# dt times the input on VectorE out of PSUM, a uniform four-state add on GpSimd, and a third softplus at a place of its own, in a scan on one Trainium2 core

## The chip, the cores and the metric

The kernel runs on one core of a Trainium2 chip. The core has five engines with a queue each: TensorE (PE: matmuls, with PEld for its weight loads), VectorE (DVE), ScalarE (ACT), GpSimd (POOL) and SyncE (SP, which only issues DMAs here). Each takes its instructions in the order in which the program gives them, and a semaphore wait holds up everything behind it on the same engine. The metric is the time of one execution in device microseconds.

## The reference, cut to what matters

The network has four layers on 8 images of 192 channels by 64 x 64 pixels. Layers 0 and 2 hold a selective scan in four directions; layers 1 and 3 have no recurrence. The change is in the scan alone, which runs 16 times (8 images, 2 layers). For each direction, with R rows that are projected to `dt` and N = 16 states:

```python
dt = softplus(einsum('kcr,bkrl->bkcl', dt_proj_w, dts) + dt_proj_b)
A = -exp(A_log)
def step(h, inp):
    dt_t, B_t, C_t, x_t = inp
    h = h * exp(dt_t[..., None] * A) + (dt_t * x_t)[..., None] * B_t[:, :, None, :]
    return h, einsum('bkcn,bkn->bkc', h, C_t)
```

So per position and channel: one softplus, one product dt x input, 16 exponentials (the decay), 16 products with B, a recurrence for each of 16 states, 16 products with C, and the sum over the 16 states. All of it is float32.

## The kernel before

**Tiling.** `scan_layer` (lines 99 to 449) works on units. A unit is 128 channel rows (block v = 0, 1 or 2; block 2 holds the last 64 channels of two directions) by Q = 512 positions; it has 4 sub-blocks of 128 positions, and its states are the tile `da` of 128 x (4 x 16 x 128) floats. Three units, v = 0, 1, 2, share one stretch of positions and make a chunk. A scan has two directions d of 8 chunks, so 16 chunks or 48 units; the whole kernel has 768 units and 256 chunks.

**What one unit costs each engine.**
- ACT: `steps_b` (L217) takes the softplus of the projected dt out of a PSUM bank into `dts`; `decay` (L244) makes the 16 exponentials of 128 x 512; `turn` copies (L231, L234) bring the transposed product into SBUF; `cut` (L253, L254) saves and clears the first column of each sub-block. Softplus and Exp are in different function tables, so the change from one to the other needs an ACT_TABLE_LOAD.
- POOL: `steps_c` (L221) makes `dtx` = dt x input. `times_c` (L317 to L322) multiplies a sub-block's 16 states by C (L319, 128 x 2048) and then adds the last n states to others (L322), so that fewer are left for PE: n = 4 in the first two sub-blocks, n = 3 in the last two.
- PE: `turn` transposes `dtx` (L229); `fill` (L287) makes dtx x B for half a sub-block into a PSUM tile `u`, of which there are two; `add_up` (L337) sums the states into `py` by matmuls with the identity, 12 for a unit, and one of half width (L342) for the state that POOL left out in two sub-blocks. `py` has one buffer.
- DVE: `scan` (L303, L305, L308) runs the recurrence on half a sub-block, 128 x 1024, in place on `da`, 8 times a unit; `diagonals_b` (L196) spreads B for the next chunk, 4 times a chunk; `finish` (L352 in direction 0, L356 in direction 1) takes `py` out.

**The order.** It is written by hand (`tc.manual_schedule()`): no scheduler moves anything. The loop at L394 takes a unit k in eight slots j. A slot issues scan(k, j), the POOL work of the sub-block behind it, `fill` for the next slot, then the rest: `finish` of unit k-2 and `turn` of unit k+1 in slot 2, `add_up` for unit k-1 with as many matmuls as SUM[v][j] says, and a part of the decay of unit k+1 (DECAY). What prepares the next chunk is spread over the three units: `steps_a` (PE, the projection of dt, into a `misc` PSUM bank, of which there are two) for two units in slot 4 of v = 0; then, in slot 1 of v = 1, one burst of three softplus with the third `steps_a` in its midst, since that one needs a bank that the first softplus frees.

**The start of a scan** (L369 to L393) makes dt, dtx, the B diagonals and the decay of unit 0 before the loop. The decay of unit 0 is made in two halves of the sub-blocks, so that DVE can begin its first scans after the first half.

**What limits how far an engine may run ahead.** `fill` for slot j+1 needs the `u` tile of slot j-1, so that scan must be over. The first matmul of `add_up` for unit k-1 needs `finish` of unit k-2 (the one buffer of `py`) and POOL's product for the last sub-block of unit k-1. The decay of unit k+1 needs the third buffer of `da`, so the last `add_up` of unit k-2.

Of the kernel before, what the change touches and what calls it, by code (L numbers as in the profile page):

```python
# [7 lines left out]
F32 = mybir.dt.float32  # L8
AF = mybir.ActivationFunctionType
ALU = mybir.AluOpType  # L10
# [4 lines left out]
P = 128  # L15
# [5 lines left out]
Q = 512  # L21
NS = 16
SB = 128
NB = Q // SB
# [16 lines left out]
def tile_net(ctx: ExitStack, tc: tile.TileContext, a: dict, out: bass.AP):  # L41
    nc = tc.nc
# [56 lines left out]
    def scan_layer():  # L99
# [5 lines left out]
        with (  # L105
# [9 lines left out]

            nck = T // Q


            NP = 12
            units = [  # L120
                (d, i, i if d == 0 else nck - 1 - i, v)
# [59 lines left out]
            def diagonals_a(m, o):  # L181

                pt = misc()
                rows = slice(o * CB, o * CB + NS)
                for i, cols in windows():
                    nc.tensor.transpose(  # L186
                        pt[:, i * NS : (i + 1) * NS], xd[m][rows, cols], ident[rows, rows]
                    )
                bts[m, o] = pt[:, : 8 * NS].rearrange("p (i n) -> p i n", n=NS)
                dg[m, o] = sw.tile([P, 8, NS // 2, 32], F32, tag=f"dg{o}", name=f"dg{o}")  # L190
# [13 lines left out]
            def steps_a(k):  # L204

                d, i, c, v = units[k]
                x = xd[k // 3][:, 0:Q]
                pz = pzs[k] = misc()
                if v < 2:
                    r = slice(v * CB, (v + 1) * CB)  # L210
                    nc.tensor.matmul(pz, wdt[r, d, 0, :], x[r], start=True, stop=True)
                else:
                    nc.tensor.matmul(pz, wdt[:, d, 1, :], x, start=True, stop=True)  # L213

            def steps_b(k):
                dts[k] = sw.tile([P, Q], F32, tag="dt", name="dt", bufs=4)
                nc.scalar.activation(dts[k], pzs.pop(k), AF.Softplus)  # L217

            def steps_c(k):
                dtx[k] = sw.tile([P, Q], F32, tag="dtx", name="dtx")  # L220
                nc.gpsimd.tensor_tensor(dtx[k], dts[k], vt[k // 3][:, units[k][3], :], ALU.mult)  # L221

            def turn(k):

# [92 lines left out]
            def times_c(k, g):  # L317
                h = das[k][:, NB - 1 - g if units[k][0] else g]
                nc.gpsimd.tensor_tensor(h, h, cts.pop((k, g)), ALU.mult)  # L319
                n = NS - NP if g < 2 else NS - NP - 1  # L320
                to = h[:, NP - n : NP]
                nc.gpsimd.tensor_tensor(to, to, h[:, NS - n : NS], ALU.add)  # L322

            def load_y(k):
                d, i, c, v = units[k]
# [6 lines left out]
            def add_up(count):  # L332

                for k, n in to_add[:count]:
                    if n == 0:
                        py[k] = sp.tile([P, Q], F32, tag="py", name="py")
                    nc.tensor.matmul(  # L337
                        py[k], ident, das[k][:, :, n, :], start=(n == 0), stop=(n == NP - 1)
                    )
                    if n == 8:  # L340
                        s = slice(0, NB // 2) if units[k][0] else slice(NB // 2, NB)
                        nc.tensor.matmul(  # L342
                            py[k][:, s.start * SB : s.stop * SB], ident, das[k][:, s, NP, :],
                            start=False, stop=False,
                        )
                del to_add[:count]

            def finish(k):
# [10 lines left out]
            nu, nm = len(units), len(units) // 3  # L359


            SUM = ((1, 0, 1, 2, 0, 2, 1, 2), (2, 2, 1, 1, 1, 2, 2, 2), (2, 1, 1, 2, 2, 2, 2, 2))
            DECAY = {2: (0, 3), 3: (3, 7), 4: (7, 9), 5: (9, 12), 6: (12, 16)}

            def has(k):
                return 0 <= k < nu
# [7 lines left out]
            load_v(1)  # L374
            steps_b(0)
            steps_c(0)
            steps_a(2)
            steps_b(1)
            diagonals_a(0, 0)
            steps_b(2)  # L380
            for r in range(2):
                diagonals_b(0, 0, r)
                load_c(0, r)
# [1 line left out]
            for s in (slice(0, NB // 2), slice(NB // 2, NB)):  # L385
                decay(0, 0, NS, s)
                cut(0, s)
                if s.start == 0:
                    steps_c(1)
                    diagonals_a(0, 1)  # L390
                    fill(0, 0)
            for r in range(2):
                diagonals_b(0, 1, r)  # L393
            for k in range(nu + 2):  # L394
                m, v = divmod(k, 3)
                ahead = 0 <= m + 1 < nm
                for j in range(8):
                    if v == 1 and j == 3 and 0 <= m + 2 < nm:
                        load_v(m + 2)
                    if has(k):  # L400
                        scan(k, j)
                    if j == 7:
                        if has(k + 1):
                            cut(k + 1)
                        if has(k):
                            keep(k)
                    if j % 2 == 0:
                        kk, g = (k, j // 2 - 1) if j else (k - 1, 3)
                        if has(kk):
                            times_c(kk, g)  # L410
                        if has((4 * kk + g + 3) // 4):
                            load_c(*divmod(4 * kk + g + 3, 4))
                    if j == 5 and has(k + 2):
                        steps_c(k + 2)
                    kk, jj = (k, j + 1) if j < 7 else (k + 1, 0)
                    if has(kk):
                        fill(kk, jj)
                    if j == 2:
                        if has(k - 2):
                            finish(k - 2)  # L420
                        if has(k - 1):
                            load_y(k - 1)
                        if has(k + 1):
                            turn(k + 1)
                    if ahead and (v, j) == (0, 4):

                        steps_a(k + 3)
                        steps_a(k + 4)
                    if ahead and v == 1 and j == 1:

                        steps_b(k + 2)
                        steps_a(k + 4)
                        steps_b(k + 3)
                        steps_b(k + 4)
                    if v == 0 and ahead:
                        if j == 0:
                            project_a(m + 1)
                        if j == 1:
                            project_b(m + 1)
                    if v > 0 and ahead:  # L440
                        if j == (5, 1)[v - 1]:
                            diagonals_a(m + 1, v - 1)
                        if j >= 6:
                            diagonals_b(m + 1, v - 1, j - 6)
                    if j == 2 and has(k - 1):
                        to_add += [(k - 1, n) for n in range(NP)]
                    add_up(SUM[v][j])
                    if has(k + 1) and j in DECAY:
                        decay(k + 1, *DECAY[j])
# [853 lines left out]
```

## Time and profile before

| | |
|---|---|
| median of 3 runs | 26363.84 us (26362.46 to 26368.85) |
| the profiled execution, its own time | 26345.77 us |
| its span, first to last instruction | 26344.0 us |
| busy: PE / DVE / ACT / POOL | 88% / 78% / 54% / 73% |
| granted TensorE clock, mean | 0.929 |
| one scan, first `xd` to the last `finish` | 1186 to 1196 us, 16 of them |
| between two scans | 435 to 465 us |
| one chunk of three units in mid-scan | 72.0 to 72.2 us |

The busy shares are means over two kinds of stage: the 16 scans, some 72% of the span, and the layers between them, in which POOL is mostly idle. A question about the scan is answered from stretches inside a scan, and there from the order of instructions on each engine. In the rows of a timeline the first figure is the start in us from the beginning of the span, the second how long the row lasts; x is the number of instructions that it merges (an fp32 matmul of PE stands as two records), and the bracket is the idle time ahead of it with what ended it. Instructions of one engine overlap a little, so the cost of one in a full queue is the distance from its start to the next one's start.

### The profile page before, as it was taken

What the parts mean: (1) busy time and instruction counts of PE and PEld (TensorE: products, weight loads), DVE (VectorE), ACT (ScalarE), POOL (GpSimd) and SP (SyncE); (2) the same over time, 40 slices, a digit from 0 to 9 for tenths busy, and PEclk for the clock granted to TensorE, in tenths of its full rate; (3) what the DMA queues carried; (4) which work ended last, traced back from release to release, by engine and by line L of the source; (5) the groups of instructions that cost most, each with busy time, mean ns of one, the idle gap of its engine ahead of it and who ended that gap; (6) DMA issues with size and microseconds to landing.
All of it is one profiled execution on the core that took longest, in us unless ns stands there. A gap on an engine that the chain in (4) does not pass through costs nothing.

```text
span 26344.0 us, 431326 instructions
## 1 busy us (share of the span) xinstructions
PE 23298.1 (88%) x173960; PEld 12085.3 (46%) x173960; DVE 20617.9 (78%) x21237; ACT 14204.8 (54%) x23120; POOL 19170.7 (73%) x7452
## 2 busy tenths in 40 slices
PE   9979889798897988979889898898989989899896
PEld 4535445353453534535345353453535535355353
DVE  7959789597885968859688696886968869688695
ACT  5646456464554645546455464554645546465463
POOL 7929589295892958939589395893958939588395
PEclk9989999899998999989999899998999989999898
DMA  5636556265563655636556365563656636566364
GB/s 168 206 92 201 148 174 205 92 203 149 171 201 96 203 145 175 200 96 202 143 177 205 93 203 139 181 201 93 203 137 182 200 96 204 134 186 197 99 204 119
DMA packets 1204798, 4293.86 MB, mean 163 GB/s; under 512 B 360224, under 2 KB 419456, under 8 KB 804480
## 3 DMA queue, kind: packets, MB, share of 16 engines
q1 hardware_dynamic: 1202816, 4266.25, 54.7%
q8 instruction: 1388, 22.74, 0.4%
q14 instruction: 594, 4.87, 0.1%
HBM read 3810.55 MB, written 450.72 MB: 162 GB/s over the span
## 4 chain that ended last, share of the span: by engine, by line
POOL 36%; PE 12%; DVE 7%; ACT 3%; issue 3%; DMA 2%; SPq 0%; POOLq 0%; DVEq 0%; ACTq 0%
POOL da L319 27%; POOL da L322 6%; PE py L337 3%; PE pa L501 2%; POOL dtx L221 2%; PE u L287 2%; DVE da L308 2%; PE pa L504 1%; ACT da L244 1%; DVE pwc L932 1%; DVE t L966 1%; DMA a<-t 1%; DMA t<-u 0%; PE paa L501 0%; PE pb L511 0%
## 5 line engine op out<-in xcount | busy, mean ns | idle before, releaser
L308 DVE TENSOR_TENSOR_SCAN da<-da,u 128x1024 f32<-128x1024 f32 x6144 | 14039.6, 2286 | 328.7 <-ACT da L254 37.9
L319 POOL TENSOR_TENSOR da<-da,ct 128x2048 f32<-128x2048 f32 x3072 | 13928.8, 4534 | 330.6 <-DVE tmp L303 302.2
L337 PE MATMUL py<-da,ident 128*128 128x512 f32 x18432 | 9494.1, 628 | 538.8 <-POOL da L319 437.4
L287 PEld LDWEIGHTS u<-dg,dtt 32*128 32x128 f32 x131072 | 5946.8, 163 | 4601.3 <-issue 4301.7
L244 ACT ACTIVATE da<-dt,neg_a 128x512 f32<-128x512 f32 (+1 forms) x12544 | 7662.2, 699 | 16.2
L287 PE MATMUL u<-dg,dtt 32*128 32x128 f32 x131072 | 7237.6, 283 | 118.0 <-DVE da L308 49.3
L337 PEld LDWEIGHTS py<-da,ident 128*128 128x128 f32 x18432 | 3122.1, 191 | 3138.8 <-issue 2239.7
L221 POOL TENSOR_TENSOR dtx<-dt,vt 128x512 f32<-128x512 f32 x768 | 979.5, 1276 | 4011.7 <-ACT dt L217 3747.0
L322 POOL TENSOR_TENSOR da<-da 128x512 f32<-128x512 f32 (+1 forms) x3072 | 3487.6, 1135 | 240.9
L231 ACT COPY dtt<-misc 128x512 f32<-128x512 f32 x768 | 450.4, 586 | 3338.3 <-PE misc L229 3338.3
L305 DVE TENSOR_TENSOR u<-u,tmp 128x8 f32<-128x8 f32 x5952 | 1007.6, 169 | 1092.7 <-PE u L287 869.8
L234 ACT COPY dtt<-misc 32x512 f32<-32x512 f32 x3008 | 1734.7, 577 | 45.2
L196 DVE TENSOR_TENSOR dg<-msk,misc 128x1024 f32<-128x1024 f32 x1024 | 1222.6, 1197 | 442.6 <-PE misc L186 258.7
L160 ACT ACTIVATE xd<-misc,msk 128x512 f32<-128x512 f32 x256 | 175.7, 686 | 1791.3 <-PE misc L156 1791.3
L217 ACT ACTIVATE dt<-misc 128x512 f32<-128x512 f32 x768 | 430.8, 595 | 1105.1 <-PE misc L213 1098.0
L914 PE MATMUL pwc<-t,l3taps 128*128 128x486 f32 (+1 forms) x1280 | 595.3, 614 | 234.4 <-DVE t L935 214.0
L920 POOL TENSOR_TENSOR acc<-u,gate 128x486 f32<-128x486 f32 (+1 forms) x80 | 108.4, 1360 | 949.5 <-DVE u L935 674.0
L876 POOL MEMSET t<- 128x4356 f32 (+2 forms) x32 | 100.6, 3145 | 934.3 <-DVE t L850 913.4
L501 PE MATMUL pa<-sqa,mean_w 128*128 128x512 f32 x384 | 306.5, 944 | 337.1 <-ACT sqa L541 337.1
L229 PE MATMUL misc<-ident,dtx 128*128 128x128 f32 x3072 | 594.2, 318 | 0.0
L186 PE MATMUL misc<-ident,xd 16*128 16x16 f32 x4096 | 565.6, 266 | 25.2 <-DVE dg L196 25.2
L186 PEld LDWEIGHTS misc<-ident,xd 16*128 16x128 f32 x4096 | 528.2, 210 | 92.6 <-issue 88.8
(286 smaller groups left out, 18307.8 us busy)
## 6 DMA issues: line engine op xcount, KB each, us to landing
ct<-cd SPq DMA_DIRECT2D x2048, 1024.0 KB
ct<-cd SPq DMA_DIRECT2D x2048, 512.0 KB
vt<-vs SPq DMA_DIRECT2D x768, 256.0 KB
yp<-yo SPq DMA_DIRECT2D x384, 256.0 KB
yo<-yp SPq DMA_DIRECT2D x384, 256.0 KB
ys<-yo SPq DMA_DIRECT2D x384, 256.0 KB
yt<-ys SPq DMA_DIRECT2D x96, 512.0 KB
t<-ys SPq DMA_DIRECT2D x96, 512.0 KB
```

The lines of the kernel that those rows point to most:

```text
L186: nc.tensor.transpose(pt[:, i * NS : (i + 1) * NS], xd[m][rows, cols], ident[rows, rows])
L196: nc.vector.tensor_tensor(dg[m, o][:, at], msk[:, 0:32].unsqueeze(1).unsqueeze(1).to_broadcast(shape), bts[m, o][:, at, r * 8 : r * 8 + 8] ...
L221: nc.gpsimd.tensor_tensor(dtx[k], dts[k], vt[k // 3][:, units[k][3], :], ALU.mult)
L234: (nc.scalar.copy if k else nc.vector.tensor_copy)(dtt[k][q * 32 : (q + 1) * 32, 1], pt[r * 32 : (r + 1) * 32])
L244: nc.scalar.activation(das[k][:, s, n, :], dts[k].rearrange("p (s t) -> p s t", t=SB)[:, s], AF.Exp, scale=neg_a[:, v, d, n : n + 1],)
L287: nc.tensor.matmul(u[ch, r * 4 : r * 4 + 4, e::4], dtt[k][rows, r, e, ch], dg[k // 3, o][rows, r * 4 + e, n], start=True, stop=True,)
L305: nc.vector.tensor_tensor(head, head, tmps[k][:, n], ALU.add)
L308: nc.vector.tensor_tensor_scan(h, h, u.rearrange("p n t -> p (n t)")[:, way], 0.0, ALU.mult, ALU.add)
L319: nc.gpsimd.tensor_tensor(h, h, cts.pop((k, g)), ALU.mult)
L322: nc.gpsimd.tensor_tensor(to, to, h[:, NS - n : NS], ALU.add)
L337: nc.tensor.matmul(py[k], ident, das[k][:, :, n, :], start=(n == 0), stop=(n == NP - 1))
L501: nc.tensor.matmul(pa[:, h], w[0][:, c], src[0][:, h], start=True, stop=False)
```

## The change

- `steps_b` makes the softplus twice: into `dts` for the decay as before, and once more in place in its PSUM bank. The bank is now freed by `steps_c`.
- `steps_c` moves from POOL to DVE: `dtx` = bank x input, with three buffers where there were two. For the next chunk's v = 0 and v = 1 both products stand in slot 2 of v = 1, ahead of `finish`; that of v = 2 stands in slot 5 of v = 2. Before, POOL made one in slot 5 of every unit.
- `times_c` adds four states in every sub-block, 128 x 512. The half-width matmul of `add_up` is gone. SUM is shifted a little.
- The third `steps_a` and softplus leave the burst: they go to slots 3 and 4 of v = 2, between parts of that unit's decay; so there is a table load to Softplus and one back twice a chunk, where it was once. `dts` has three buffers where it had four.
- `turn` stands in slot 3 for v = 1.
- At the start of a scan the projection, softplus and product of unit 2 come behind the decay of unit 0; the softplus and product of unit 2 and the second B diagonals stand ahead of the first scan, in this order on DVE.

In the numbering of the changed file the lines from 216 on differ by up to 6.

```diff
--- before.py
+++ after.py
@@ -213,12 +212,14 @@
                     nc.tensor.matmul(pz, wdt[:, d, 1, :], x, start=True, stop=True)
 
             def steps_b(k):
-                dts[k] = sw.tile([P, Q], F32, tag="dt", name="dt", bufs=4)
-                nc.scalar.activation(dts[k], pzs.pop(k), AF.Softplus)
+
+                dts[k] = sw.tile([P, Q], F32, tag="dt", name="dt", bufs=3)
+                nc.scalar.activation(dts[k], pzs[k], AF.Softplus)
+                nc.scalar.activation(pzs[k], pzs[k], AF.Softplus)
 
             def steps_c(k):
-                dtx[k] = sw.tile([P, Q], F32, tag="dtx", name="dtx")
-                nc.gpsimd.tensor_tensor(dtx[k], dts[k], vt[k // 3][:, units[k][3], :], ALU.mult)
+                dtx[k] = sw.tile([P, Q], F32, tag="dtx", name="dtx", bufs=3)
+                nc.vector.tensor_tensor(dtx[k], pzs.pop(k), vt[k // 3][:, units[k][3], :], ALU.mult)
 
             def turn(k):
 
@@ -317,9 +318,8 @@
             def times_c(k, g):
                 h = das[k][:, NB - 1 - g if units[k][0] else g]
                 nc.gpsimd.tensor_tensor(h, h, cts.pop((k, g)), ALU.mult)
-                n = NS - NP if g < 2 else NS - NP - 1
-                to = h[:, NP - n : NP]
-                nc.gpsimd.tensor_tensor(to, to, h[:, NS - n : NS], ALU.add)
+                to = h[:, 2 * NP - NS : NP]
+                nc.gpsimd.tensor_tensor(to, to, h[:, NP:NS], ALU.add)
 
             def load_y(k):
                 d, i, c, v = units[k]
@@ -337,12 +337,6 @@
                     nc.tensor.matmul(
                         py[k], ident, das[k][:, :, n, :], start=(n == 0), stop=(n == NP - 1)
                     )
-                    if n == 8:
-                        s = slice(0, NB // 2) if units[k][0] else slice(NB // 2, NB)
-                        nc.tensor.matmul(
-                            py[k][:, s.start * SB : s.stop * SB], ident, das[k][:, s, NP, :],
-                            start=False, stop=False,
-                        )
                 del to_add[:count]
 
             def finish(k):
@@ -359,7 +353,7 @@
             nu, nm = len(units), len(units) // 3
 
 
-            SUM = ((1, 0, 1, 2, 0, 2, 1, 2), (2, 2, 1, 1, 1, 2, 2, 2), (2, 1, 1, 2, 2, 2, 2, 2))
+            SUM = ((1, 0, 1, 2, 0, 2, 1, 2), (2, 2, 1, 2, 2, 2, 2, 2), (1, 0, 1, 2, 2, 2, 2, 2))
             DECAY = {2: (0, 3), 3: (3, 7), 4: (7, 9), 5: (9, 12), 6: (12, 16)}
 
             def has(k):
@@ -374,10 +368,9 @@
             load_v(1)
             steps_b(0)
             steps_c(0)
-            steps_a(2)
             steps_b(1)
             diagonals_a(0, 0)
-            steps_b(2)
+            steps_c(1)
             for r in range(2):
                 diagonals_b(0, 0, r)
                 load_c(0, r)
@@ -386,9 +379,11 @@
                 decay(0, 0, NS, s)
                 cut(0, s)
                 if s.start == 0:
-                    steps_c(1)
-                    diagonals_a(0, 1)
+                    steps_a(2)
                     fill(0, 0)
+            steps_b(2)
+            steps_c(2)
+            diagonals_a(0, 1)
             for r in range(2):
                 diagonals_b(0, 1, r)
             for k in range(nu + 2):
@@ -410,8 +405,11 @@
                             times_c(kk, g)
                         if has((4 * kk + g + 3) // 4):
                             load_c(*divmod(4 * kk + g + 3, 4))
-                    if j == 5 and has(k + 2):
+                    if v == 1 and j == 2 and ahead:
                         steps_c(k + 2)
+                        steps_c(k + 3)
+                    if v == 2 and j == 5 and ahead:
+                        steps_c(k + 3)
                     kk, jj = (k, j + 1) if j < 7 else (k + 1, 0)
                     if has(kk):
                         fill(kk, jj)
@@ -420,18 +418,20 @@
                             finish(k - 2)
                         if has(k - 1):
                             load_y(k - 1)
-                        if has(k + 1):
-                            turn(k + 1)
+                    if j == (2, 3, 2)[v] and has(k + 1):
+                        turn(k + 1)
                     if ahead and (v, j) == (0, 4):
 
                         steps_a(k + 3)
                         steps_a(k + 4)
-                    if ahead and v == 1 and j == 1:
-
+
+                    if ahead and (v, j) == (1, 1):
                         steps_b(k + 2)
-                        steps_a(k + 4)
                         steps_b(k + 3)
-                        steps_b(k + 4)
+                    if ahead and (v, j) == (2, 3):
+                        steps_a(k + 3)
+                    if ahead and (v, j) == (2, 4):
+                        steps_b(k + 3)
                     if v == 0 and ahead:
                         if j == 0:
                             project_a(m + 1)
```

## The prediction

> **What bounds the kernel now.** I read four views: busy time in stretches, groups with their shapes, timelines of single engines inside a scan, and the timeline of a scan's start. First the stretches, since the shares of the whole span mix scans with the layers between (columns: stretch, length, busy time and instructions of PE, PEld, DVE, ACT, POOL, granted clock, DMA):
>
> ```profile
> 204.00:1332.00 1128.00, 1092.21 (x9809) 628.42 (x9808) 1033.32 (x1031) 707.37 (x1214) 1113.26 (x423) 0.99 0.67 203
> ```
>
> Inside the first scan POOL is busy 98.7% of the time, but PE 96.8% and DVE 91.6% too; only ACT (62.7%) has room. Three engines stand within 7% of each other, so what is taken from POOL counts only until the next one is full. One unit on POOL:
>
> ```profile
> 613.72 4.53 POOL L319 TENSOR_TENSOR da<-da,ct 128x2048 f32<-128x2048 f32 x1
> 618.32 0.99 POOL L322 TENSOR_TENSOR da<-da 128x384 f32<-128x384 f32 x1
> 619.27 4.53 POOL L319 TENSOR_TENSOR da<-da,ct 128x2048 f32<-128x2048 f32 x1
> ...
> 635.28 1.27 POOL L322 TENSOR_TENSOR da<-da 128x512 f32<-128x512 f32 x1
> 636.51 1.26 POOL L221 TENSOR_TENSOR dtx<-dt,vt 128x512 f32<-128x512 f32 x1
> ```
>
> No row has idle time. The next L319 stands at 637.74, so a unit is 24.02 us and a chunk 72.07: POOL sets the pace. Over all scans the time between the first scan instructions of successive chunks is 71.94 in the mean for chunks 2 to 15, 74.71 for the first (PE's clock is at half until about 50 us after a scan's start).
>
> The same chunk on DVE runs from 614.97 to 687.04. Brackets with idle time sum to some 3.3 us there (0.3 of 21.8 us in v = 0, 1.95 of 25.6 in v = 1, 1.0 of 24.7 in v = 2), so DVE needs 68.76 without them. PE's idle brackets are 0.83 + 0.50 + 0.89, so PE needs 69.85.
>
> **The change part by part, in a chunk.**
>
> POOL. It loses three products and has two wider sums in each unit:
>
> ```profile
> L322 POOL TENSOR_TENSOR da<-da 128x512 f32<-128x512 f32 x1536 | 1957.5, 1274 | 120.5
> L322 POOL TENSOR_TENSOR da<-da 128x384 f32<-128x384 f32 x1536 | 1530.1, 996 | 120.4
> L196 DVE TENSOR_TENSOR dg<-msk,misc 128x1024 f32<-128x1024 f32 x1024 | 1222.6, 1197 | 442.6 <-PE misc L186 258.7 <-DMA vt<-vs 183.5
> L342 PE MATMUL py<-da,ident 128*128 128x256 f32 x1536 | 456.9, 379 | 0.0
> L217 ACT ACTIVATE dt<-misc 128x512 f32<-128x512 f32 x768 | 430.8, 595 | 1105.1 <-PE misc L213 1098.0 <-PE misc L211 4.2
> L217 ACT ACT_TABLE_LOAD x256 | 328.4, 1283 | 12.6 <-PE misc L211 8.3
> L356 DVE TENSOR_TENSOR yo<-yo,py 128x512 f32<-128x512 f32 x384 | 257.5, 671 | 277.8 <-PE py L337 277.8
> ```
>
> By starts, L221 takes 1.23 and each wider sum adds 0.28: 24.02 - 1.23 + 0.56 = 23.35 a unit, 70.05 a chunk. That alone would gain 2.0. `steps_c` issues no DMA; the loads of C on SP still wait for L319 alone, and no row of L319 inside a scan waits for them.
>
> PE. It loses L342 three times, 0.5 each by the distance of starts: 69.85 - 1.5 = 68.35.
>
> DVE. It gains three products of 128x512 with one operand in PSUM. The row of L356 is the same operation with the same kinds of operands: 671 ns, 0.58 from start to start in a full queue; the costlier L352 takes 0.64. I take 0.60 (bounds 0.55 and 0.75): 68.76 + 1.80 = 70.56. In direction 1 `finish` is L356 and saves 0.06 three times, 0.09 in the mean of both: 70.47. So DVE, not POOL, is the fullest engine afterwards, with nothing yet for its waits.
>
> DVE's waits. They come from PE, by way of `finish`. In a chunk of the first scan where POOL is not yet the limit:
>
> ```profile
> 264.94 0.72 DVE L352 SCALAR_TENSOR_TENSOR yo<-vt,skip,py 128x512 f32<-128x512 f32 x1
> ...
> 271.04 0.17 DVE L305 TENSOR_TENSOR u<-u,tmp 128x8 f32<-128x8 f32 x1 [0.17 <-PE u L287]
> ```
> ```profile
> 265.81 1.10 PE L337 MATMUL py<-da,ident 128*128 128x512 f32 x2 [0.80 <-DVE u L305]
> 266.83 1.16 PE L287 MATMUL u<-dg,dtt 32*128 32x128 f32 x16
> 267.92 1.98 PE L337 MATMUL py<-da,ident 128*128 128x512 f32 x4
> 269.84 1.16 PE L287 MATMUL u<-dg,dtt 32*128 32x128 f32 x16
> ```
>
> PE stands idle 0.80 until `finish` has emptied the only `py`, 0.87 after its start; so in slot 2 PE loses whatever lead it had. From there it must do one add (1.02), fill (1.09), two adds (1.92) and the next fill (1.16) before DVE's scan of slot 5 may begin, while DVE does `finish` and the scans of slots 3 and 4: 0.64 + 2.52 + 2.69 = 5.85. PE: 0.87 + 1.02 + 1.09 + 1.92 + 1.16 + 0.05 to reach DVE = 6.11. The wait is 0.26; rows of this spot in v = 0 show 0.17 to 0.33. After the change every unit has this spot, since DVE and no longer POOL is late in slot 2. Into the same stretch of PE the change puts `turn` for v = 1 (0.58: wait 0.84, and about 0.2 more in slot 6 behind the diagonals) and the third `steps_a` for v = 2 (0.96, less 0.2 for that block's shorter fills and the add behind it: wait 1.0). Sum 0.26 + 1.04 + 1.0 = 2.3. In v = 1 the two products stand ahead of `finish`, so PE waits some 1.6 us for them too; this moves both engines alike and adds no wait. The chunk is 70.47 + 2.3 = 72.8 against 71.94: **0.86 slower**.
>
> ACT. A second softplus per unit (L217, 595 ns; in place in PSUM it is not shown: 0.54 by its step to 0.69 by L160's row, I take 0.55) and one more pair of table loads (2 x 1.283) in a chunk. In v = 1 nothing is near: softplus ends some 4 us before DVE asks. In v = 2 the load, the softplus and the load stand between the exponentials: `turn` ends 7.1 us after DVE began the unit, copies 2.95, 16 exponentials at 0.62, two loads 2.57, two softplus 1.1, `cut` 0.62 = 24.3, and DVE needs the next unit's decay at 25.3. Cover 1.0 us; the product of slot 5 is ready at 16.8, asked for at 17.5, cover 0.7; behind that product on DVE stand the scans of slots 6 and 7 and the diagonals, and POOL waits for those scans. So I cost ACT at nothing; if that cover is gone, each us is 256 us on the whole.
> [...]
>
> **The start of a scan.**
>
> ```profile
> 5074.79 6.50 ACT L244 ACTIVATE da<-dt,neg_a 128x256 f32<-128x256 f32 x16
> ...
> 5081.73 6.48 ACT L244 ACTIVATE da<-dt,neg_a 128x256 f32<-128x256 f32 x16
> ```
> ```profile
> 5077.09 2.35 DVE L196 TENSOR_TENSOR dg<-msk,misc 128x1024 f32<-128x1024 f32 x2
> 5081.85 4.46 DVE L308 TENSOR_TENSOR_SCAN da<-da,u 128x1024 f32<-128x1024 f32 x2 [2.41 <-ACT da L254]
> 5088.48 0.18 DVE L303 TENSOR_TENSOR tmp<-da,da 128x16 f32<-128x16 f32 x1 [2.17 <-ACT da L253]
> ```
>
> DVE begins after the first half of the decay. After the change the product of unit 2 stands ahead on DVE, and its softplus on ACT behind both halves: ACT reaches 5088.2, table load 1.28, two softplus 1.1, product 0.65, second diagonals 2.25: the first scan at 5093.5, **11.7 later**. This wait holds DVE's whole queue, and POOL and PE behind it. In the first chunk the 2.17 for the second half go and the three products come (1.8): together nothing, within 3 either way by the half clock. At the end POOL follows DVE more closely: 2 less.
>
> **The sum.** Per scan 11.7 + 14 x 0.86 - 2 = 21.7; 16 scans: 347. The profiled execution took 26345.8: 26693. It lies 18 below the median of the runs, so against these I say **26710** (+1.3%). The layers between the scans keep their code.
>
> **Rivals** (on the runs' scale; about 0.2%, 53 us, is what a measurement of this kernel can tell from no change).
> A, faster: PE's two `u` tiles carry it over slot 5 and DVE has no waits. A chunk is then 70.5, 1.44 less than before: 11.7 - 20 - 2 = -10.5 a scan, 26195. For it: PE's work is lower than DVE's in every unit. Against: the `finish` bracket, which takes the lead away once a unit. It decides where the waits fall below 0.8 a chunk (11.7 - 2 = 14 x 0.69).
> B, the pace stays and only the start is late: 9.7 a scan, 26520. For it: stalls near 1.5.
> C, ACT loses its cover in v = 2: with softplus in PSUM 0.15 dearer and each step's semaphore, 1 us beyond the cover gives 26970.
> D, the change doesn't do what it says and POOL still sets the pace: 70.05 + DVE's hand-over, which ends as A or at no change. Its idle-free rows speak against: they get shorter by 0.67 a unit whatever else happens.
>
> **How the numbers follow.** Forecast 60%, B 15%, C 8%, A and D together 17%, of which 7 end within 0.2%. The forecast's own range: the product at 0.55 to 0.75 gives -34 to +100 and the waits at 1.6 to 2.9 a chunk -157 to +134: 26520 to 26900 (not both upper ends at once). To hold 8 in 10 it reaches down over B: 26400 to 26900. Slower 0.83, within 0.2% 0.07, faster 0.10.
>
> **What would show it.** POOL with idle rows ahead of its products in mid-scan; DVE without idle but for L305 waiting on PE in slot 5, least in v = 0; PE's first add of each unit waiting for `finish`; a mid-scan chunk of 72.5 to 73.2; the first scan instruction of a scan some 28 us after its first `xd` (16 to 18 before). It is wrong if DVE waits for ACT in v = 2, if the product of 128x512 is not near 0.6, or if the waits on `fill` vanish.

## The result, and the profile after

The changed kernel takes 28427.86 us (median of 4 runs, 28419.2 to 28432.71) where the kernel before takes 26366.35 beside it: a ratio of 1.0783, 95% interval 1.077 to 1.0796. It is slower, as forecast, but by 2060 us and not by 350; 26400 to 26900 does not hold it.

The first view again, the same stretch of the first scan in the changed kernel (length; busy time and instructions of PE, PEld, DVE, ACT, POOL; granted clock; DMA):

```profile
204.00:1332.00 1128.00, 1062.34 (x8861) 602.81 (x8860) 969.60 (x984) 722.36 (x1203) 989.22 (x343) 0.90 0.60 185
```

POOL is no longer full (87.7%), as forecast, but nor is DVE (86.0%), which was to take its place. In the same 1128 us DVE got through 984 instructions, before 1031. The column to look at is the clock: 0.90 where it was 0.99. Over the whole run it goes from 0.929 to 0.867.

By stages: from the first `xd` to the last `finish` a scan takes 1318.2 us in the mean, before 1190.2. Sixteen times 128.0 is 2048, nearly all of the 2085 by which the two profiled spans differ. The first chunk is 77.85 (74.71), chunks 2 to 15 are 79.66 in the mean (71.94; single ones lay between 70.8 and 74.4, wider than the 72.0 to 72.2 of the table above); by blocks v = 0, 1, 2 these are 22.66, 28.43, 28.58 (21.80, 25.60, 24.55).

POOL's timeline in mid-scan, where before no row had idle time:

```profile
636.66 4.55 POOL L320 TENSOR_TENSOR da<-da,ct 128x2048 f32<-128x2048 f32 x1 [3.23 <-DVE tmp L304]
641.29 1.27 POOL L322 TENSOR_TENSOR da<-da 128x512 f32<-128x512 f32 x1
643.23 4.52 POOL L320 TENSOR_TENSOR da<-da,ct 128x2048 f32<-128x2048 f32 x1 [0.68 <-ACT carry L316]
...
665.31 4.54 POOL L320 TENSOR_TENSOR da<-da,ct 128x2048 f32<-128x2048 f32 x1 [4.10 <-DVE tmp L304]
```

POOL waits for scans. What DVE waits for, from the groups (the last part of a row is idle time ahead of it, with its releasers):

```profile
L306 DVE TENSOR_TENSOR u<-u,tmp 128x8 f32<-128x8 f32 x5952 | 1015.0, 171 | 2589.2 <-PE u L288 2377.8
L222 DVE TENSOR_TENSOR dtx<-misc,vt 128x512 f32<-128x512 f32 x768 | 496.0, 672 | 636.9 <-ACT misc L218 511.3
```

The new product is 672 ns, the 671 of the row it was priced by. Its waits on ACT are nearly all at scan starts (509 of the 511 us). DVE waits 2378 us for `fill` on PE (870 before). So what is PE doing? Its timeline around slot 2 of one unit, v = 2:

```profile
650.37 0.75 PE L230 MATMUL misc<-ident,dtx 128*128 128x128 f32 x4
652.79 1.56 PE L337 MATMUL py<-da,ident 128*128 128x512 f32 x2 [1.67 <-DVE u L306]
654.28 1.98 PE L288 MATMUL u<-dg,dtt 32*64 32x128 f32 x32
656.20 2.08 PE L212 MATMUL misc<-xd,wdt 128*128 128x512 f32 x2
658.06 2.90 PE L337 MATMUL py<-da,ident 128*128 128x512 f32 x4
660.89 1.10 PE L288 MATMUL u<-dg,dtt 32*64 32x128 f32 x32
```

PE stands idle 1.67 us until `finish` (L346, the second row below) has emptied `py`; the bracket names the short L306 that ends right behind it.

```profile
649.71 2.29 DVE L309 TENSOR_TENSOR_SCAN da<-da,u 128x1024 f32<-128x1024 f32 x1
651.92 0.72 DVE L346 SCALAR_TENSOR_TENSOR yo<-vt,skip,py 128x512 f32<-128x512 f32 x1
652.55 0.17 DVE L306 TENSOR_TENSOR u<-u,tmp 128x8 f32<-128x8 f32 x1
```

Then everything is slow: this `fill` takes 1.98 and the next 1.10; two adds take 2.90 where they took 1.98. The same moment by stretches shows why:

```profile
649.90:653.30 3.40, 1.73 (x26) 1.15 (x18) 3.37 (x4) 2.11 (x4) 3.40 (x1) 1.00 1.10 248
653.30:660.10 6.80, 6.80 (x39) 3.42 (x38) 4.38 (x4) 6.73 (x11) 6.64 (x4) 0.50 0.76 180
660.10:663.50 3.40, 3.40 (x38) 1.55 (x37) 1.40 (x2) 3.37 (x6) 1.11 (x1) 1.00 0.80 311
```

Behind 3.4 us in which PE was busy for 1.73, the granted clock is 0.50 for 6.8 us. DVE pays at once:

```profile
656.33 0.17 DVE L306 TENSOR_TENSOR u<-u,tmp 128x8 f32<-128x8 f32 x1 [1.08 <-PE u L288]
656.54 2.29 DVE L309 TENSOR_TENSOR_SCAN da<-da,u 128x1024 f32<-128x1024 f32 x1
662.06 0.17 DVE L306 TENSOR_TENSOR u<-u,tmp 128x8 f32<-128x8 f32 x1 [3.23 <-PE u L288]
```

From here on "bracket" is such an idle time of PE, "mid-scan" begins 60 us after a scan's first scan instruction, and a "half stretch" is a time at clock 0.50 there. Mid-scan ends with a scan's last scan instruction. Before, it has 32 half stretches (249 us), 30 of them in the last chunk of a scan, and of PE's 695 brackets over 0.25 us 668 are under 1.4. After, it has 503 (3751 us), 471 of them ahead of the last chunk, and 649 of 797 brackets are between 1.4 and 1.9; those ahead of a unit's first add are 1.47, 1.50 and 1.58 in the mean of v = 0, 1, 2.

Last, the start of a scan on DVE:

```profile
3723.54 0.69 DVE L222 TENSOR_TENSOR dtx<-misc,vt 128x512 f32<-128x512 f32 x1 [14.14 <-ACT misc L218]
3724.14 2.34 DVE L195 TENSOR_TENSOR dg<-msk,misc 128x1024 f32<-128x1024 f32 x2
3726.40 4.46 DVE L309 TENSOR_TENSOR_SCAN da<-da,u 128x1024 f32<-128x1024 f32 x2
```

Product, diagonals, first scan, in the order forecast. From the first `xd` to the first scan instruction it is 28.3 us in the mean, before 16.6: 11.7 later.

### The profile page after: what moved, and what is told of

It is laid out like the page before. It is cut to its first block, busy times and chain, and to the rows that moved or that the text cites. A ratio compares the mean times of both kernels' runs of the same rounds, so it can differ in the third digit from the quotient of the medians.

```text
span 28429.2 us, 429911 instructions
## 1 busy us (share of the span) xinstructions
PE 24493.1 (86%) x172424; PEld 12571.0 (44%) x172424; DVE 21099.8 (74%) x22005; ACT 15315.6 (54%) x24400; POOL 18679.4 (66%) x6684
## 4 chain that ended last, share of the span: by engine, by line
PE 59%; DVE 24%; issue 7%; ACT 5%; DMA 3%; POOL 2%; SPq 1%; DVEq 0%; POOLq 0%; ACTq 0%
PE py L337 26%; PE u L288 17%; DVE da L309 11%; PE pa L501 3%; DVE dg L195 2%; ACT da L245 2%; PE misc L212 2%; PE pa L504 2%; DVE u L306 1%; DVE dtx L222 1%; PE misc L230 1%; DVE pwc L932 1%; PE misc L210 1%; DVE yo L346 1%; PE misc L152 1%
## 5 line engine op out<-in xcount | busy, mean ns | idle before, releaser
L337 PE MATMUL py<-da,ident 128*128 128x512 f32 x18432 | 10230.9, 675 | 1130.0 <-DVE u L306 1084.5
L288 PEld LDWEIGHTS u<-dg,dtt 32*128 32x128 f32 x131072 | 6336.3, 173 | 5125.0 <-issue 4861.9
L288 PE MATMUL u<-dg,dtt 32*128 32x128 f32 x131072 | 7687.5, 297 | 208.1 <-DVE da L309 113.3
L337 PEld LDWEIGHTS py<-da,ident 128*128 128x128 f32 x18432 | 3434.4, 208 | 4308.4 <-issue 3985.7
L322 POOL TENSOR_TENSOR da<-da 128x512 f32<-128x512 f32 x3072 | 3894.6, 1268 | 240.9
L306 DVE TENSOR_TENSOR u<-u,tmp 128x8 f32<-128x8 f32 x5952 | 1015.0, 171 | 2589.2 <-PE u L288 2377.8
L245 ACT ACT_TABLE_LOAD x512 | 656.9, 1283 | 907.1 <-PE py L337 901.9
L222 DVE TENSOR_TENSOR dtx<-misc,vt 128x512 f32<-128x512 f32 x768 | 496.0, 672 | 636.9 <-ACT misc L218 511.3
L316 ACT COPY carry<-da 128x16 f32<-128x16 f32 x672 | 145.8, 217 | 1375.8 <-DVE da L309 1374.8
L145 PE MATMUL misc<-vt,wxt 128*128 128x512 f32 x512 | 311.6, 693 | 430.7 <-DMA vt<-vs 245.2
L217 ACT ACT_TABLE_LOAD x512 | 656.9, 1283 | 17.2 <-PE misc L210 8.3
L230 PE MATMUL misc<-ident,dtx 128*128 128x128 f32 x3072 | 664.9, 348 | 0.0
```

Source lines behind the costliest of these rows:

```text
L222: nc.vector.tensor_tensor(dtx[k], pzs.pop(k), vt[k // 3][:, units[k][3], :], ALU.mult)
L230: nc.tensor.transpose(pt[:, i * P : (i + 1) * P], dtx[k][:, cols], ident)
L245: nc.scalar.activation(das[k][:, s, n, :], dts[k].rearrange("p (s t) -> p s t", t=SB)[:, s], AF.Exp, scale=neg_a[:, v, d, n : n + 1],)
L288: nc.tensor.matmul(u[ch, r * 4 : r * 4 + 4, e::4], dtt[k][rows, r, e, ch], dg[k // 3, o][rows, r * 4 + e, n], start=True, stop=True,)
L306: nc.vector.tensor_tensor(head, head, tmps[k][:, n], ALU.add)
L322: nc.gpsimd.tensor_tensor(to, to, h[:, NP:NS], ALU.add)
```

## The experiments

The theory from these views, CLOCK: the late `finish` gives PE an idle bracket of 1.5 us once a unit, the granted clock falls to half behind it, and the chunk is longer because PE is slow then. The main rival, ORDER: the chain of products, `finish`, adds and fills is longer by itself, and the clock only follows. Later CLOCK was split: IDLE (only idle time counts) and FULLWORK (a stretch with too little work of the whole array counts, idle or not). All medians, ratios to the kernel before run beside each, and what mid-scan looks like:

| run | edit on the changed kernel | us | ratio (95%) | chunk | half stretches (us) |
|---|---|---|---|---|---|
| before | | 26366.35 | | 71.94 | 32 (249) |
| after | none | 28427.86 | 1.0783 (1.077 to 1.0796) | 79.66 | 503 (3751) |
| e1 | a fill repeated in the bracket | 27404.02 | 1.0401 (1.0386 to 1.0417) | 75.17 | 148 (1591) |
| e2 | half a fill repeated | 28098.48 | one run | 78.15 | 362 (3079) |
| e8 | a full matmul ahead of that fill | 27108.86 | 1.0291 (1.0275 to 1.0306) | 73.77 | 33 (372) |
| e7 | `finish` earlier | 26499.87 | 1.0063 (1.0046 to 1.0079) | 71.77 | 183 (894) |
| e5 | start of a scan mended | 28236.55 | 1.0718 (1.0702 to 1.0734) | 79.88 | 513 (3871) |
| e13 | e7 and e5 | 26322.5 | 0.9993 (0.9984 to 1.0002) | 71.68 | 183 (891) |
| e9 | the old SUM | 28784.08 | 1.0931 (1.0914 to 1.0948) | 81.82 | 432 (4854) |
| e15 | the old sum of states on POOL | 28165.71 | 1.0692 (1.0676 to 1.0708) | 78.72 | 376 (3099) |
| e3 | two `py`, da0 in SBUF | 29418.44 | 1.1165 (1.1147 to 1.1184) | 84.6 | 460 (4669) |
| e4 | da0 in SBUF alone | 30434.02 | one run | 88.34 | 688 (6564) |
| e11 | **the kernel before**, `finish` longer | 27136.02 | 1.03 (1.0284 to 1.0315) | 74.96 | 229 (1802) |
| e17, e12, e18, e19 | e13 and PE's order in v = 2 | see below | | | |

**Work put into the bracket (e1, e2).** The fill of slot 3 is made twice; the second time changes nothing in the result.

```diff
                     if j == (2, 3, 2)[v] and has(k + 1):
                         turn(k + 1)
+                    if j == 2 and has(kk):
+                        fill(kk, jj, us[kk, jj], range(4))   # e2: range(2)
```

> The changed kernel, but PE makes the products dtx x B of slot 3 a second time in slot 2 (the same matmuls into the same tile, 1.09 us, behind turn), where it otherwise stands idle 1.5 to 1.7 us until finish. This adds PE work and takes no wait of any engine away. Theory CLOCK (the idle time in slot 2 brings TensorE's granted clock to half for 3.4 to 10 us in the middle of a scan, 503 times, and PE at half rate holds DVE up): the gap falls to about 0.5 us, which in neither trace brings the half clock (0 of 528 gaps of 0.4 to 0.9 us before), the half-clock stretches in mid-scan fall below 60, a chunk takes about 73 us and the run 26600 to 26900. Rival QUEUE (the clock only follows; the loop is long because of DVE's three products and ACT's second softplus and table loads): no faster than 28400, rather slower by the added matmuls.

> As e1, but only half of the matmuls are repeated (0.55 us), so that a gap of about 1.0 us is left. CLOCK, with the counts of gaps in the two traces (around 1.0 us: 15 of 128 before, 11 of 20 after are followed by the half clock; around 1.5 us 339 of 536; from 1.75 us nearly all): some 50 to 200 half-clock stretches in mid-scan, 26700 to 27400. QUEUE: 28400 or more.

More work for PE, and the kernel is 1024 us faster: ORDER has no room for that. With half of it (one run) the bracket is about 1.0 and 362 half stretches are left, more than the 50 to 200 expected, and the time is above its range too. And e1 gives back only half of the loss, outside its range. Of its 148 half stretches 118 have no bracket over 1.2 us ahead; they come in v = 2 where PE does only fills (32 rows), 16-row transposes and the turn for 5.5 us in the mean, the short bracket included. So it is not idle time alone.

**The same bracket, filled by the whole array (e8).**

```diff
+                if j == 3:
+                    nc.tensor.matmul(u[:, 0:4, :], ident, vt[k // 3][:, v, :], start=True, stop=True)
                 n = slice(j % 2 * 4, j % 2 * 4 + 4)
```

The product is thrown away, since the fill overwrites it.

> The changed kernel with one more full matmul (128x128 by 512 columns) once a unit, into the tile that the fill of slot 3 then overwrites (so its product is thrown away); the idle bracket in slot 2 is filled up to some 0.6 us, as with the repeated fill, but by work of the whole array instead of 32 rows. CLOCK as refined by the repeated fill (what counts is how much full-array work stands in a stretch of some 3.4 us, not idle time alone): fewer half-clock stretches than the 148 of the repeated fill, those of v = 2 gone too, chunk 72.8 to 74.5, 26650 to 27100. IDLE (any work counts alike): as the repeated fill, 27300 to 27500. ORDER: 0.5 to 0.96 more PE work in a unit, so 28400 to 29000.

33 half stretches, 31 of them in last chunks, where the kernel before has 32 and 30; and the chunk falls to 73.77 although PE has one more full matmul a unit. That is FULLWORK, against IDLE's 27300 to 27500. The total is 9 us above the range; the first chunk is 80.24 there (77.85 in the changed kernel).

**The bracket taken away (e7).** `finish` moves ahead of the point where PE needs `py`; the instructions are the same.

```diff
                     if has(k):
                         scan(k, j)
+                    if j == (1, 2, 1)[v] and has(k - 2):
+                        finish(k - 2)
...
                     if j == 2:
-                        if has(k - 2):
-                            finish(k - 2)
```

> The changed kernel with finish moved ahead of the sums' next turn: in v = 0 and v = 2 behind the scan of slot 1, in v = 1 behind the scan of slot 2 but ahead of the two products. The instructions of every engine are the same in kind and number. CLOCK (an idle bracket of PE of about 1.5 us or more, once a unit, brings the granted clock to half for 6.8 us, and that lengthens the chunk from 72.8 to 79.7): the brackets ahead of the first add fall under 1 us, half-clock stretches in mid-scan from 503 to 100 to 200 (those of v = 2, slot 2, where PE has no add for 5 us, stay), chunk 73 to 75.5, 26700 to 27400. ORDER (the chunk is longer because the products, finish and fills follow each other in a longer chain, and the clock only follows): DVE's and PE's work is the same, so 28200 to 28500.

1928 us of the 2060 are back by moving one instruction a unit; DVE's wait for `fill` is 411 us instead of 2378. The chunk, 71.77, is under that of the kernel before. Both are below what CLOCK had expected (73 to 75.5, and 26700 to 27400). The 151 half stretches that have no bracket over 1.2 us ahead were foreseen; one of them on PE:

```profile
322.43 1.10 PE L288 MATMUL u<-dg,dtt 32*64 32x128 f32 x32
323.46 1.13 PE L185 MATMUL misc<-ident,xd 16*128 16x16 f32 x8
324.76 1.22 PE L288 MATMUL u<-dg,dtt 32*64 32x128 f32 x32 [0.17 <-DVE da L309]
325.91 1.13 PE L230 MATMUL misc<-ident,dtx 128*128 128x128 f32 x4
326.84 1.91 PE L337 MATMUL py<-da,ident 128*128 128x512 f32 x2
```
```profile
322.20:325.60 3.40, 3.23 (x73) 2.77 (x72) 3.26 (x6) 0.00 (x0) 3.32 (x2) 1.00 0.62 135
325.60:329.00 3.40, 3.40 (x25) 1.60 (x21) 3.33 (x4) 1.89 (x4) 3.40 (x2) 0.50 0.92 231
```

PE is busy 3.23 of 3.40 us, nearly all of it with matmuls that use 32 and 16 rows, and the clock is halved all the same: PE's busy share does not show it.

**The bracket put into the kernel before (e11).** One more read of `py` ahead of `finish`, into a tile that nothing reads.

```diff
                 p, y = py.pop(k), yo.pop(k)
+                y2 = sw.tile([P, Q], F32, tag="y2", name="y2", bufs=1)
+                nc.vector.tensor_tensor(y2, vt[k // 3][:, v, :], p, ALU.add)
```

> The kernel before with one more VectorE operation ahead of finish that also reads py (the sum goes to a scratch tile that nothing reads), some 0.65 us, so that PE's idle bracket of 0.8 us in slot 2 becomes some 1.45 us; nothing else is changed. CLOCK: half-clock stretches in mid-scan from 32 to 200 or more, 26900 to 28000. ORDER: DVE's work goes from 68.76 to 70.7 in a chunk, still under POOL's 72.07, so 26340 to 26550.

```profile
609.70 1.68 PE L337 MATMUL py<-da,ident 128*128 128x512 f32 x2 [1.16 <-DVE u L305]
611.31 1.99 PE L287 MATMUL u<-dg,dtt 32*64 32x128 f32 x32
613.22 3.78 PE L337 MATMUL py<-da,ident 128*128 128x512 f32 x4
```

0.65 us on an engine that had room costs 3.0% without any part of the change: the same mechanism, in the other kernel. Here a bracket of 1.16 was enough (half clock from 610.1).

**The start (e5), and both mended (e13).** e5 leaves out the early `steps_c(2)` and issues it in slot 2 of the first unit.

> The changed kernel, but the product dt x input of unit 2 stands in slot 2 of unit 0 and no longer ahead of the first scan on DVE. The prediction's price for this start is 11.7 us a scan: CLOCK and QUEUE both expect the first scan instruction 10 to 12 us earlier against the first xd, and 28230 to 28330 in all, a ratio of 0.994 to 0.997 to the changed kernel's 28427.9. If the lateness is made up later in the scan: 28400.

> The changed kernel with finish moved ahead as in the run e7, and with the third block's first product and diagonals out of the way of the first scan as in the run e5. If the two losses (the half clock behind the late finish, and the start of a scan) are separate, they add: 26500 less 191 is 26310, between 26250 and 26370 (about the kernel before: 0.996 to 1.001). If the start is hidden once the chunks are shorter, 26450 to 26510.

e5 is 191 us below the changed kernel by its median (12 a scan); the first scan comes 16.1 us after the first `xd` again. The two losses add: with both gone the change can't be told from the kernel before (0.9993, 0.9984 to 1.0002). Chunks 2 to 15 are 0.26 shorter, the first is 77.44, 2.7 longer.

**Parts of the change undone (e9, e15).** e9 has the old SUM; e15 has the old `n` in `times_c` and the half-width matmul back.

> The changed kernel with the old division of the adds over the slots (v = 1 gives two adds from slots 3 and 4 to slots 0 and 1 of v = 2). CLOCK: the bracket of 1.5 us ahead of the first add of each unit stays, so most half-clock stretches stay; those of v = 2 without a bracket may go: 400 to 503 stretches, 28000 to 28450. SUMORDER (the new division of the adds is itself the loss): 26600 to 27100.

> The changed kernel with the sum of states as before (GpSimd three states in half of a unit, the half-width matmul back), the products on VectorE and all else of the change left. CLOCK: the late finish and its bracket of 1.5 us are still there and PE has 0.5 more work in a unit, so 28300 to 28800. POOLSUM (the wider sums on GpSimd are what costs): 26600 to 27200.

Neither is the loss; both totals miss their ranges. In e9 389 of 421 brackets of 1.375 to 1.625 us are followed by half clock (in the changed kernel 339 of 536), and 221 more brackets wait for the turn's copies: it is slower than the changed kernel. In e15 PE has more work and the kernel is 262 us faster than the changed one, since PE comes later to slot 2 and its bracket is shorter (411 of 784 are between 0.875 and 1.375, in the changed kernel 39 of 797). That was not foreseen, but it has CLOCK's sign.

**Two buffers for `py` (e3), and its control (e4).** To make room in PSUM for a second `py`, da0 goes to SBUF; e4 does only that.

```diff
-            da0 = sp.tile([P, 2, NB, NS], F32, name="da0")
+            da0 = sw.tile([P, 2, NB, NS], F32, name="da0", bufs=1)
-                        py[k] = sp.tile([P, Q], F32, tag="py", name="py")
+                        py[k] = sp.tile([P, Q], F32, tag="py", name="py", bufs=2)   # e3 only
```

> The changed kernel, but py has two buffers (da0 moves from PSUM to SBUF for it), so that the first add of slot 2 no longer waits for finish. CLOCK: PE's gaps of 1.5 us go, and with them both the half clock and the 2.3 us per chunk that DVE waits on fill: a chunk of about 71.1 us, which with the scan's start 11.7 us later gives 26300 to 26500. QUEUE: the products and the softplus are still there, 27500 or more.

> The changed kernel with da0 in SBUF instead of PSUM, nothing else (the control for the run e3, where py had two buffers too). PORT (a VectorE operation with both inputs in SBUF does not end before GpSimd's running instruction): tmp <- da0, da/carry takes up to 4.5 us instead of 0.17 in hundreds of places and the time is 28700 to 29800. OTHER (the second py was the cause in e3): tmp stays at 0.2 us and 28430 within 60.

e3 fell far outside. The control (one run, itself above its range) shows why: the move of da0 alone costs 2000 us, and the second `py` gives 1000 of it back. `tmp <- da0, carry`, with both inputs in SBUF now, takes 2917 ns in the mean instead of 161. All 653 that began while a POOL instruction ran ended 0.03 us behind it; the 19 others took 0.15. One of them on DVE, and POOL's instruction of that moment:

```profile
631.48 3.83 DVE L304 TENSOR_TENSOR tmp<-da,carry 128x16 f32<-128x16 f32 x1
```
```profile
630.78 4.50 POOL L320 TENSOR_TENSOR da<-da,ct 128x2048 f32<-128x2048 f32 x1 [0.65 <-ACT carry L316]
```

Both end at 635.3. So e3 says little on `py`; e7 is the clean test.

**The rest in v = 2 (e17, e12, e18, e19).** All are e13 with one add moved from v = 1 to v = 2, to shorten PE's stretch without a full-array matmul there: to slot 1 (e17), to slot 0 (e12), to slot 1 with that add ahead of the 16-row transposes (e19), and with the add of slot 2 ahead of the turn as well (e18). In e17, e18 and e19 `finish` is issued behind the add of slot 1, since that is now the last one into the `py` that it empties.

```diff
-            SUM = ((1, 0, 1, 2, 0, 2, 1, 2), (2, 2, 1, 2, 2, 2, 2, 2), (1, 0, 1, 2, 2, 2, 2, 2))
+            SUM = ((1, 0, 1, 2, 0, 2, 1, 2), (2, 2, 1, 1, 2, 2, 2, 2), (1, 1, 1, 2, 2, 2, 2, 2))  # e12: 2, 0
```

> The changed kernel with finish ahead (e7), the start mended (e5), and one add moved from slot 3 of v = 1 to slot 1 of v = 2, where PE in e7 works 4.4 us without idle time on fills (32 rows), 16-column transposes and the turn alone and the granted clock falls to half. FULLWORK (a stretch of 3.4 us with too little full-array work drops the clock, idle or not): the some 150 half-clock stretches without a bracket ahead in mid-scan of e7 and e13 fall under 60, chunk 70.5 to 71.5, 26050 to 26260. IDLE (only brackets of idle time drop it): the stretches stay, 26280 to 26400.

> As e13 (finish ahead, start mended), and one add moved from slot 3 of v = 1 to slot 0 of v = 2, so that py is whole before slot 1 and finish has no wait on PE as in e17. FULLWORK: PE's stretch without a full-array add in v = 2 goes from 3.5 to some 3.1 us (to the turn), half-clock stretches without a bracket fall from 153 to under 60, chunk 70.8 to 71.4 against 71.68 in e13, 26120 to 26270, faster than the kernel before. IDLE: the stretches stay, 26280 to 26370.

> As e17 (finish ahead, start mended, one add moved to slot 1 of v = 2), and in v = 2 the add of slot 1 ahead of the 16-column transposes and the add of slot 2 ahead of the turn. PE's longest stretch without a full-array matmul in v = 2 is then some 2.2 us (diagonals' transposes and one fill) instead of 3.5 to 4.7, and finish does not wait for the add. FULLWORK: half-clock stretches without a bracket under 40, chunk 70.6 to 71.4, 26090 to 26260, faster than the kernel before. IDLE: 130 to 153 stretches stay, 26300 to 26400. If finish still waits, 26450 or more.

> As e18, but the turn of v = 2 stays ahead of the add of slot 2, so that steps_a of slot 3 does not wait for the turn's copies. FULLWORK: the stretch without a full-array add in v = 2 is some 3.7 us of fill, transposes and turn, half of that without the turn; half-clock stretches 40 to 110, chunk 70.9 to 71.6, 26150 to 26310. If the stretch is still long enough for the clock, as e13: 26300 to 26340. A new wait as in e17 or e18: 26450 or more.

| run | us | ratio (95%) | chunk | half stretches, of them without a bracket over 1.2 | new wait in v = 2 |
|---|---|---|---|---|---|
| e13 | 26322.5 | 0.9993 (0.9984 to 1.0002) | 71.68 | 183, 153 | |
| e17 | 26584.01 | 1.0098 (1.0082 to 1.0115) | 72.65 | 84, 40 | `finish` 1.0 for PE's add |
| e12 | 26365.54 | 1.0015 (1.0006 to 1.0024) | 71.84 | 172, 132 | |
| e18 | 26842.22 | 1.0193 (1.0179 to 1.0207) | 73.56 | 176, 0 | `steps_a` 2.0 for ACT |
| e19 | 26462.97 | 1.0035 (1.0023 to 1.0048) | 72.15 | 46, 0 | `steps_a` 1.1 for ACT |

The stretch of v = 2 without an add or projection on PE is 4.0 us in the mean in e13 and still 4.0 in e12, since the next add comes behind a fill that waits for DVE's scan; so e12 does not test it, and its 132 half stretches stayed. In e17 and e19 it is 2.6, and of 153 half stretches without a bracket 40 and 0 are left: there FULLWORK is right and IDLE is not. In e18 there is none either, but 129 stand behind the new bracket of 2.0, so it shows nothing on this. But no order gains, and all four times lie above what FULLWORK expected: in e18 and e19 `steps_a` needs the bank that the turn's copies on ACT free,

```profile
394.06 1.57 PE L212 MATMUL misc<-xd,wdt 128*128 128x512 f32 x2 [2.00 <-ACT dtt L235]
```

(e18). In e19, where only 15 half stretches are left ahead of the last chunks, the wait of 1.1 stands there and the chunk is 72.15, longer than in e13. None of these runs beats the kernel before.

**The clock from the rows.** In the kernel before and the changed one 2184 of 2186 stretches at one clock last a multiple of 3.413 us, and in nine of the runs the half stretches begin on a grid of 3.413 us (mean distance 0.004 us). For each grid period of mid-scan at full clock I summed PE's time in matmuls of 64 or 128 rows, plus 0.3 of the time in fills and 16-row transposes; the 0.3 is a fit, of five weights from 0.1 to 0.3 the one that parts the first four traces best. It is not sharp: 0.35 parts these four worse, and the other five alone would give 0.2. How many periods were followed by half clock:

| sum in 3.413 us | after, e7, e11, e18 | before, e8, e12, e13, e19 (not fitted) |
|---|---|---|
| under 1.12 us | 256 of 256 | 180 of 180 |
| 1.12 to 1.38 | 571 of 579 | 196 of 206 |
| 1.38 to 1.62 | 261 of 792 | 87 of 675 |
| over 1.62 | 1 of 17664 | 3 of 24009 |

## Why the prediction was wrong

**Right.** POOL has idle rows in mid-scan and is not the bound (in the chain that ended last its share falls from 36% to 2%). The product costs 672 ns, 0.60 to the next instruction's start in the rows of a scan's start, as forecast. Every unit's first add waits for `finish`. DVE waits for ACT's softplus at scan starts and 2.2 us elsewhere in the whole run, so rival C did not occur. A change to Softplus cost ACT its load of 1283 ns and hardly more, as the prediction priced it: ahead of all 1536 softplus stands 9.3 us of idle time together, and 17.2 ahead of the 512 loads to Softplus. A scan starts 11.7 later, as worked out. The rest of DVE's sum is not contradicted: with the bracket gone (e7) the chunk is 71.77, between rival A's 70.5 and the forecast 72.8. One cover was too generous: at that pace (e7) DVE does wait for the softplus in slot 5 of v = 2, in 197 chunks, some 0.35 us each, where 0.7 to spare had been counted.

That the change is slower was forecast, and the start alone, which the sum had priced, would have made it so (191 us by e5; e7, where most of the loss by the clock is gone, is still 0.63% slower). But nearly all of the 2060 us is a term that the sum did not have, so the forecast sign says little for its working in the chunk.

**Wrong: the chunk.** Forecast 72.8, measured 79.66: 6.9 too little, times 14 times 16 is 1540 us of the 1700 missing. The first chunk (3.1 longer, costed at nothing, within 3) and the last with the end (costed at -2) are the rest, some 10 us a scan together.

The step that failed is one sentence: "In v = 1 the two products stand ahead of `finish`, so PE waits some 1.6 us for them too; this moves both engines alike and adds no wait." For v = 1 the size was near (1.50 measured), and two things were not.

First, such a bracket stands in every v. The bracket of 0.80 was carried over for v = 0 and v = 2, though it was read where PE itself came late. With DVE late, PE starts the fill as soon as the scan of slot 1 ends, and DVE then needs a scan, `finish` and the semaphore, 2.5 + 0.64 + 0.15, PE a fill and a turn, 1.09 + 0.58: 1.6 us idle. Measured: 1.55 in a row of v = 0 and 1.67 in the row of v = 2 above. All these terms stand in rows of before. By the prediction's own sum this length alone would cost nothing, since its waits count from the start of `finish`.

Second, "adds no wait" took the durations of PE (1.02, 1.09, 1.92, 1.16) as fixed. They are so at full clock only: in the rows above a fill takes 1.98 for 1.10 and two adds 2.90 for 1.98. The profile of before had a sign of it, though only in the last chunk of each scan: there 23 of 26 brackets of 1.625 to 2.375 us are followed by half clock, while of all those under 0.875 in mid-scan none of 528 is. The prediction used the clock only for the first 50 us of a scan. That this is the cause is shown from both sides: without the bracket (e7) 1928 us are gone; with the array busy in it and more work (e8) the clock stays (33 half stretches, before 32) and the chunk is 73.77; with the bracket in the kernel before (e11) that one loses 3.0%.

The idle time that went ahead of half clock was short: 1.67 us in the row of v = 2 above, 1.16 in the row of e11, and 0.17 in the rows of e7, where PE was busy 3.23 of 3.40 us, nearly all of it with matmuls of 32 and 16 rows.

**What stays open.** The first chunk of a scan is 1.2, 2.7 and 5.5 longer than before in e7, e13 and e8; no run takes that apart. Whether two `py` alone would do as well as the early `finish` is not known: no run has two with da0 left in PSUM. The weight of 0.3 for matmuls of few rows is a fit, and no run varies the rows alone.

## What to carry to other kernels

An idle time on TensorE was not a loss of its own length here: behind one of 1.67 us the clock was 0.50 for 6.8 us. Look at what clock the rows behind it were granted, and sum the full-array work of each clock period around it (3.413 us in these traces), not the busy share. When a change makes another engine the late one, work the hand-overs out again from who is late then; a bracket that was read under the old order does not carry over. An operation that frees a single buffer should be issued where its input is ready, not where it is tidy: here one instruction a unit, at most one slot earlier, was worth 1928 of 28428 us.

## What the hardware showed that was not expected

- In nine traces the granted clock went to half behind nearly every period of 3.413 us whose full-array work (fills of 32 rows at the fitted 0.3) summed to less than 1.38 us (all 436 under 1.12, 767 of 785 between 1.12 and 1.38), behind 348 of 1467 between 1.38 and 1.62, and hardly ever above 1.62 (4 of 41673). In the changed kernel it stayed there for 3.4, 6.8 or 10.2 us in 483 of 503 cases. Busy time did not tell it: 3.23 of 3.40 us busy and halved (e7).
- A VectorE operation of 128x16 with both inputs in SBUF did not end before GpSimd's running instruction did (e4, 653 of 653): 161 ns became 2917 in the mean, 3.83 us in the rows shown, while the 19 that met no GpSimd instruction took 0.15 us. With one input in PSUM it did not happen: in the changed kernel 585 of the 672 such operations began and ended within one GpSimd instruction, none took over 175 ns, and all 480 products that began while GpSimd was busy ended before its instruction did, at 673 ns in the mean.
